# Row maxima of two attention stages as one stream over all units, ahead of the scores

## The chip, the cores and the metric

The kernel runs on one core of a Trainium2 chip (trn2). The metric is the device time of one execution in microseconds. The kernel before takes 6175.1 us, the median of three runs (6174.22 to 6192.93). The engines of the core are named as in the profile: PE (TensorE, matrix products), DVE (VectorE), ACT (ScalarE), POOL (GpSimd) and SP (SyncE, which only issues DMAs here). [...]

## The reference

The program is a whole decoder of four layers over 1024 tokens of 128 features. Each layer has a self-attention, a cross-attention to 6404 context rows, and a feed-forward part. Two of its twelve parts matter here. The first self-attention (layer 0) is causal, with 16 heads of size 8 and rotary positions:

```
q, k, v = x @ W_Q.T, x @ W_K.T, x @ W_V.T        (16 heads of 8, q and k rotated)
scores  = q @ k.T / sqrt(8), masked causally
x       = x + softmax(scores) @ v @ W_O.T
```

The last cross-attention (layer 3) has no causal mask, 6404 keys, and a mask over the keys:

```
q = Q @ Wq.T + bq;  k = ctx @ Wk.T + bk;  v = ctx @ Wv.T + bv
scores = where(mask == 0, -1e9, q @ k.T / sqrt(8))
ctx    = softmax(scores) @ v;   out = ctx @ Wo.T + bo
```

A softmax over 6404 keys needs the maximum of each row of scores before the exponentials. The kernel computes the scores twice: once with queries on the partitions, to find the row maxima, and once with keys on the partitions, for the exponentials and the product with the values.

## The kernel before

**Units.** Both stages work in eight units. A unit is a group of four heads (`g`, 0 to 3) and one half of the queries (`h`, 512 of them). The cross-attention takes unit n as g = n // 2, h = n % 2, the self-attention as g = n % 4, h = n // 4. A float32 query and key of size 8 are split into three bfloat16 parts, and stacked into 64 rows for each head (`split`, `pairs_read`), so one PE row group of 64 serves one head. Two heads share a tile of 128 partitions, which the code calls a pair. The key side has ones in three extra rows. Into the same rows of the query tile `qP` the negative maximum is added, as three parts, so that the second product yields scores less maximum at once.

**The maxima** of a unit come from `pairs_max`. A step is 128 queries against 512 keys for both pairs: per pair two matrix products into a PSUM tile `m2` of two banks, and one DVE reduction of 128 x 1024 scores to two maxima a row (L1275). In the cross-attention a unit has 13 chunks of keys times 4 query tiles, 52 steps; the last chunk has 260 keys. In the self-attention a unit has 4 steps in the first half of the queries and 8 in the second, with the causal mask added by two more products where a step meets the diagonal.

**The turn.** After the last step `pairs_neg` reduces over the chunks (L1285), splits the negative maximum into three parts with nine small DVE operations (L1285 to L1291) and writes them into the padded tile `mpad`. PE then turns `mpad` with four transposes for each pair (L1295), and DVE adds the result to the unit's part of `qP` (L1297).

**The scores.** `pairs_core` runs over the key tiles of a unit, 51 in the cross-attention and 4 or 8 in the self-attention. A tile has four score products into three single-bank PSUM tiles `s`, four exponentials on ACT (L1347), and four products with the values into `acc`, one tile late. The argument `beside` is the stream of steps for the next unit's maxima: the first pair of each tile is followed by one step, and what is left is run after the last tile. Then `acc` is copied to `oT`, on DVE and ACT in turn (L271, L273), and `pairs_norm` transposes it (L1368) and divides by the sums (L1371, L1373).

So the order around each boundary between units is: last value products, left-over steps, the negative maxima, the transposes of `mpad` and `oT`, the addition to `qP`, and only then the first scores of the next unit:

```
for n in range(7):
    g, h = n // 2, n % 2
    oT = pool1.tile([P, BANK], F32, tag="oT", name="oT")
    self.pairs_core(ps, pool1, qPs[g], kPs[g % 2], v, g, h, oT, AF.Exp, 64, maxima(n + 1))
```

The first unit's maxima run ahead of all scores: in the cross-attention in a prelude of 52 steps, among which `all_values` computes the values, in the self-attention in 4 steps. The eighth unit of the cross-attention has no maxima beside it and runs in a wider form (two banks to an exponential, L1344).

**What sets the order.** The matrix products made with `self.matmul` (L265) stay in the order of the program on PE. A scheduler places the rest: the small operations on DVE, the transposes, and the work of `between`, which in the self-attention replaces context rows that the first mask leaves out (L584 on DVE, L593 on ACT, L594 on POOL) and computes keys of the next stage (L599). In the cross-attention two tiles of keys `kP` serve in turn; the read of the next group is issued after the second unit of a group.

Of the kernel before, what the change touches and what calls it, by code (L numbers as in the profile page):

```python
# [10 lines left out]
F32 = mybir.dt.float32  # L11
# [3 lines left out]
AF = mybir.ActivationFunctionType  # L15
# [4 lines left out]
P = 128  # L20
# [191 lines left out]
class Decoder:  # L212
# [251 lines left out]
    def l0_attn(self):  # L464
# [9 lines left out]
        with tc.tile_pool(name="a", bufs=2) as pool:  # L474
# [41 lines left out]
            with tc.tile_pool(name="a1", bufs=2) as pool1, tc.tile_pool(name="a1_ps", bufs=2, space=PSUM) as ps0:  # L516
                ps = _Psum(ps0, m2=2, s=3, acc=1)
                steps = steps(ps)

                def maxima(n):  # L520
                    if n < 8:
                        return self.pairs_max(ps, pool1, qPs[n % 4], kPs[n % 4], n // 4, mpad, S, causal)
                    return ()

                for step in maxima(0):
                    step(0)
                    step(1)
# [725 lines left out]
    def pairs_max(self, ps, pool, qP, kP, h, mpad, nk=NK, causal=None):  # L1253
# [7 lines left out]
        for c in range(chunks):  # L1261
            for t in range(4):
                q0 = h * BANK + t * P
                a, b = c * BANK, min((c + 1) * BANK, nk if causal is None else q0 + P)

                def step(pair, a=a, b=b, q0=q0, t=t, c=c):
                    diag = causal is not None and b == q0 + P
                    m = ps.tile([P, 2, BANK], F32, tag="m2", name="m2")
                    for j in range(2):
                        r = slice(64 * j, 64 * j + 64)  # L1270
                        self.matmul(m[:, j, :b - a], lhsT=qP[pair][r, q0:q0 + P], rhs=kP[pair][r, a:b], start=True, stop=not diag)
                    if diag:
                        for j in range(2):
                            self.matmul(m[:, j, b - a - P:b - a], lhsT=causal[:, 1, :], rhs=causal[:, 0, :], start=False, stop=True)
                    nc.vector.tensor_reduce(mx[:, t, 2 * pair:2 * pair + 2, c:c + 1], m[:, :, :b - a], AX.X, ALU.max)  # L1275

                yield step
        self.pairs_neg(ps, pool, qP, h, mpad, mx)

    def pairs_neg(self, ps, pool, qP, h, mpad, mx):  # L1280

        nc = self.nc
        r = pool.tile([P, 4, 4], F32, tag="r", name="r")
        part = pool.tile([P, 4, 4], BF16, tag="part", name="part")
        nc.vector.tensor_reduce(r, mx, AX.X, ALU.max, negate=True)  # L1285
        mp = mpad.rearrange("p a t (j r) -> p t a j r", r=64)
        for i in range(3):
            nc.vector.tensor_copy(part, r)
            nc.vector.tensor_copy(mp[:, :, :, :, 7 + 8 * i], part.rearrange("p t (a j) -> p t a j", a=2))
            if i < 2:  # L1290
                nc.vector.tensor_tensor(r, r, part, ALU.subtract)  # L1291
        m = ps.tile([P, 2, BANK], F32, tag="m2", name="m2")
        for pair in range(2):
            for t in range(4):
                nc.tensor.transpose(m[:, pair, t * P:(t + 1) * P], mpad[:, pair, t, :], self.ident)  # L1295
            q = qP[pair][:, h * BANK:(h + 1) * BANK]
            nc.vector.tensor_tensor(q, q, m[:, pair, :], ALU.add)  # L1297

    def pairs_core(self, ps, pool, qP, kP, v, g, h, oT, func, rows, beside=None, between=None, causal=None):

# [20 lines left out]
        for t in range(nkt):  # L1321
# [1 line left out]
            off = 0 if causal is None else max(t * P - h * BANK, 0)  # L1323
            w, hs = BANK - off, slice(h * BANK + off, (h + 1) * BANK)
            diag = causal is not None and t >= 4 * h
            step = next(beside, None)
            ws = []
            for pair in range(2):
                both = None
# [16 lines left out]
                    for j in range(2):  # L1346
                        nc.scalar.activation(pp[j][:n, :w], ss[j][:n, :w], func)  # L1347
                ws += pp
                if step and pair == 0:
                    step(0)  # L1350
                    step(1)
            if late:
                values(*late.pop(0))
            late.append((t, n, off, ws))
            if between is not None:
                next(between, None)
        values(*late.pop(0))
        for step in beside:
            step(0)
            step(1)  # L1360
        self.copy(oT, acc)

    def pairs_norm(self, ps, pool, oT, o, g, h):
# [391 lines left out]
    def l3_xattn(self):  # L1755
# [5 lines left out]
        with tc.tile_pool(name="x", bufs=2) as pool:  # L1761
# [28 lines left out]
            with tc.tile_pool(name="x1", bufs=2) as pool1, tc.tile_pool(name="x1_ps", bufs=2, space=PSUM) as ps0:  # L1790
                ps = _Psum(ps0, m2=2, s=3, acc=1)

                def maxima(n):
                    if n < 8:
                        return self.pairs_max(ps, pool1, qPs[n // 2], kPs[n // 2 % 2], n % 2, mpad)
                    return ()
# [109 lines left out]
```

## Time and profile before

| What | us |
|---|---|
| Median of three runs | 6175.1 |
| The profiled execution, its own time | 6182.17 |
| Its span | 6180.4 |
| Granted PE clock over the span | 0.944 of full |
| First self-attention, units | 66 to 277 |
| Cross-attention, prelude of the first unit's maxima | 4870 to 4990 |
| Cross-attention, units 0 to 6 with maxima beside | 4990 to 5891 |
| Cross-attention, unit 7 alone | 5891 to 5987 |

The profile is of one execution. Times in it are counted from the start of its span. A row of the timeline gives start and length in us, engine, line and operation, the tile written and those read, partitions by elements, and a count of merged instructions; in brackets stand the idle time before it and what ended that. The table of stretches gives for each engine the busy time and the number of instructions, then the granted PE clock as a share of the full one. A line number can be that of a helper: all products made with `self.matmul` show as L265, so the tile's name tells them apart (`m` maxima, `s` scores, `acc` values).

Over the whole span PE is busy 5749.6 us, DVE 3757.0, ACT 3096.5 and POOL 2254.1. Most of that belongs to stages that the change leaves alone.

### The profile page before, as it was taken

Reading aid. Unit: us, or ns where it says so; the run is one execution under the profiler, and the core shown is the slowest. Engines: PE = TensorE matmul, PEld = TensorE weight load, DVE = VectorE, ACT = ScalarE, POOL = GpSimd, SP = SyncE. Lnnn points to the kernel's source line nnn. Section 1 sums busy time; section 2 is a strip of 40 time slices with the busy share of each in tenths; the row PEclk is TensorE's granted clock in tenths of the full one; section 3 lists DMA queues with packets and bytes.
Section 4 is the critical chain, followed back from the end, with each engine's and each line's share of the span. In section 5 each row is a group of like instructions: output and inputs, shape, how many; then the busy total and the mean of one; then the engine's idle time right before and its main releaser. Section 6 shows DMA issues by size and latency. Waiting matters only on the chain. (4 is left out here: it accounts for less than half of the span.)

```text
span 6180.4 us, 72184 instructions
## 1 busy us (share of the span) xinstructions
PE 5749.6 (93%) x29144; PEld 2078.1 (34%) x29144; DVE 3757.0 (61%) x4571; ACT 3096.5 (50%) x4041; POOL 2254.1 (36%) x1088
## 2 busy tenths in 40 slices
PE   5899999999999999999899968999989689999999
PEld 2333333333333434333476423111124311111126
DVE  6587777777777777776325552100014799999923
ACT  2434444444444444444211225899951167888872
POOL 2057767677777767678321541100001000000000
PEclk7899999999999999999979977999999689999999
DMA  3000000000000000000000013200022100000000
GB/s 113 4 1 1 1 1 1 1 1 1 1 1 1 1 1 1 1 17 18 33 1 14 0 58 87 88 11 7 1 83 80 54 1 22 1 22 1 1 6 29
DMA packets 65200, 117.97 MB, mean 19 GB/s; under 512 B 10475, under 2 KB 46673, under 8 KB 63201
## 3 DMA queue, kind: packets, MB, share of 16 engines
q1 hardware_dynamic: 64288, 110.08, 5.5%
q8 instruction: 228, 3.74, 0.3%
q10 hardware_dynamic: 576, 3.28, 0.1%
q14 instruction: 108, 0.88, 0.0%
HBM read 81.88 MB, written 31.42 MB: 18 GB/s over the span
## 5 line engine op out<-in xcount | busy, mean ns | idle before, releaser
L741 POOL TENSOR_TENSOR tot<-tot,p 128x1024 f32<-128x1024 f32 (+1 forms) x800 | 1889.8, 2362 | 584.5 <-ACT p L732 569.0
L732 ACT ACTIVATE p<-p,drop,keep 128x1024 f32<-128x1024 f32 (+1 forms) x816 | 1011.8, 1240 | 1321.7 <-DVE p L731 1260.0
L669 DVE TENSOR_REDUCE mx<-m 128x2 f32<-128x1024 f32 (+1 forms) x832 | 982.4, 1185 | 496.3 <-PE m L668 479.8
L1275 DVE TENSOR_REDUCE mx<-m 128x2 f32<-128x1024 f32 (+4 forms) x928 | 1027.1, 1159 | 93.5 <-PE m L265 82.2
L731 DVE TENSOR_TENSOR p<-s,every 128x1024 f32<-128x1024 f32 (+1 forms) x816 | 991.5, 1215 | 73.2 <-PE s L726 34.7
L1347 ACT ACTIVATE p<-s 128x512 f32<-128x512 f32 (+4 forms) x1620 | 819.7, 588 | 238.8 <-PE s L265 238.0
L668 PE MATMUL m<-kT,qT 64*128 64x512 f32 (+1 forms) x3328 | 888.6, 606 | 12.3 <-DVE mx L669 11.6
L1344 ACT ACTIVATE p<-s 128x1024 f32<-128x1024 f32 x918 | 843.9, 1185 | 31.5 <-PE s L1339 24.1
L726 PE MATMUL s<-qT,kT 64*128 64x512 f32 (+1 forms) x3264 | 837.7, 596 | 16.6 <-DVE p L731 15.4
L713 PE MATMUL acc<-p,v 128*64 128x512 f32 (+1 forms) x3264 | 809.4, 606 | 4.8 <-ACT p L732 3.8
L1318 PE MATMUL acc<-p,v 128*8 128x512 f32 (+2 forms) x3672 | 621.9, 597 | 0.0
L265 PE MATMUL m<-kP,qP 64*128 64x512 bf16 (+4 forms) x1856 | 371.5, 396 | 102.7 <-DVE mx L1275 57.0
L726 PEld LDWEIGHTS s<-qT,kT 64*128 64x128 f32 (+1 forms) x3264 | 321.7, 185 | 412.5 <-issue 342.1
L668 PEld LDWEIGHTS m<-kT,qT 64*128 64x128 f32 x3328 | 280.7, 185 | 504.1 <-DVE mx L669 371.4
L265 PE MATMUL acc<-p,v 128*9 128x512 f32 (+2 forms) x3240 | 422.2, 593 | 0.0
L265 PE MATMUL s<-qP,kP 64*128 64x512 bf16 (+4 forms) x1620 | 384.0, 387 | 8.9 <-ACT p L1347 6.2
L713 PEld LDWEIGHTS acc<-p,v 128*64 128x64 f32 (+1 forms) x3264 | 198.8, 136 | 550.9 <-issue 457.9
L1339 PE MATMUL s<-qP,kP 48*128 48x512 bf16 (+2 forms) x1836 | 281.0, 384 | 2.7 <-ACT p L1344 1.9
L271 DVE COPY oT<-acc 128x512 f32<-128x512 f32 x14 | 9.7, 690 | 404.4 <-PE acc L1318 395.7
L387 POOL MEMSET mpad<- 128x512 f32 x2 | 1.1, 529 | 641.2 <-PE m L1428 600.4
L265 PEld LDWEIGHTS <-qP 64*128 64x128 bf16 x1856 | 122.7, 96 | 319.6 <-issue 261.9
L265 PEld LDWEIGHTS <-kP 64*128 64x128 bf16 (+1 forms) x1620 | 83.7, 94 | 352.3 <-issue 347.4
(484 smaller groups left out, 4512.5 us busy)
## 6 DMA issues: line engine op xcount, KB each, us to landing
kd<-part SPq DMA_DIRECT2D x156, 128.0 KB, 1.9
wb<-expert_weights SPq DMA_DIRECT2D x30, 512.0 KB, 3.7
kP<-kd SPq DMA_DIRECT2D x24, 512.0 KB, 3.6
kP<-kd SPq DMA_DIRECT2D x48, 192.0 KB, 4.5
w_expert<-in_Y_w SPq DMA_DIRECT2D x8, 768.0 KB, 4.2
qd<-part SPq DMA_DIRECT2D x36, 128.0 KB, 1.8
qP<-qd SPq DMA_DIRECT2D x16, 256.0 KB, 6.2
ctxT<-in_ctxT ACTq DMA_DIRECT2D x4, 800.5 KB, 6.5
```

Source lines behind the costliest of these rows:

```text
L265: return self.tc.keep_in_program_order(self.nc.tensor.matmul(*a, **k))
L668: nc.tensor.matmul(m[:, j, :b - a], lhsT=qT[r, q0:q0 + P], rhs=kT[r, a:b], start=True, stop=True)
L669: tc.keep_in_program_order(nc.vector.tensor_reduce(mx[:, t, :, c:c + 1], m[:, :, :b - a], AX.X, ALU.max))
L713: nc.tensor.matmul(acc[64 * j:64 * j + 64, :], lhsT=v[:n, t, 64 * j:64 * j + 64], rhs=pr[:n, j, :], start=t == 0, stop=t == NKT - 1, tile_ ...
L726: nc.tensor.matmul(s[:n, j, :], lhsT=kT[r, t * P:t * P + n], rhs=qT[r, hs], start=True, stop=True)
L731: tc.keep_in_program_order(nc.vector.tensor_tensor(pr[:n], s[:n], every[:n], ALU.add))
L732: nc.scalar.activation(pr[:n], pr[:n], AF.Exp, bias=drop[:n, t:t + 1], scale=keep[:n, t:t + 1])
L741: nc.gpsimd.tensor_tensor(tot[:n], tot[:n], pr[:n], ALU.add)
L1275: nc.vector.tensor_reduce(mx[:, t, 2 * pair:2 * pair + 2, c:c + 1], m[:, :, :b - a], AX.X, ALU.max)
L1318: matmul(acc[32 * j:32 * j + v.shape[3], off:], lhsT=v[:n, t, 4 * g + j, :], rhs=ws[j][:n, :BANK - off], start=t == 0, stop=t == nkt - 1, ...
L1344: nc.scalar.activation(p2[:n], both[:n], func)
L1347: nc.scalar.activation(pp[j][:n, :w], ss[j][:n, :w], func)
```

## The change

The steps of all eight units become one stream. `pairs_max` no longer runs the turn at its end: it returns its steps and a function that starts it. `pairs_neg` does the small DVE operations when called and returns a second function, `turned`, with the transposes and additions. A new function, `maxima_of`, joins the units: after the last step of a unit it issues the small operations, then yields the next unit's first step, and issues `turned` after it. The transposes of `mpad` now stay in program order on PE.

`pairs_core` takes the stream and a number of steps for the unit and spreads these over its tiles. With 52 steps over 51 tiles the last tile has two, the second of them after its second pair. Nothing is left over at the end of a unit.

The stream starts early: in the cross-attention 56 steps run in the prelude, 52 of the first unit and 4 of the second, and every unit then takes 52 (the seventh finds 48). In the self-attention 6 run ahead, and the units take 4, 4, 6, 8, 8, 8, 8 and 8 as far as there are any. A unit's turn thus comes inside the unit before it: in the cross-attention in front of the second maxima of the tile that has the first step of the unit after.

```diff
-                def maxima(n):
-                    if n < 8:
-                        return self.pairs_max(ps, pool1, qPs[n % 4], kPs[n % 4], n // 4, mpad, S, causal)
-                    return ()
-
-                for step in maxima(0):
+                maxima = self.maxima_of(self.pairs_max(lambda: ps, pool1, qPs[n % 4], kPs[n % 4], n // 4, mpad, S, causal)
+                                        for n in range(8))
+                for _ in range(6):
+                    step = next(maxima)
                     step(0)
                     step(1)
...
-                    self.pairs_core(ps, pool1, qPs[g], kPs[g], v, g, h, oT, AF.Exp, 64, maxima(n + 1), steps, causal)
+                    self.pairs_core(ps, pool1, qPs[g], kPs[g], v, g, h, oT, AF.Exp, 64,
+                                    (maxima, 4 if n < 2 else 6 if n == 2 else 8), steps, causal)
...
-        self.pairs_neg(ps, pool, qP, h, mpad, mx)
+        return steps(), lambda: self.pairs_neg(banks, pool, qP, h, mpad, mx)
...
-        m = ps.tile([P, 2, BANK], F32, tag="m2", name="m2")
-        for pair in range(2):
-            for t in range(4):
-                nc.tensor.transpose(m[:, pair, t * P:(t + 1) * P], mpad[:, pair, t, :], self.ident)
-            q = qP[pair][:, h * BANK:(h + 1) * BANK]
-            nc.vector.tensor_tensor(q, q, m[:, pair, :], ALU.add)
+
+        def turned():
+            m = banks().tile([P, 2, BANK], F32, tag="m2", name="m2")
+            for pair in range(2):
+                for t in range(4):
+                    self.tc.keep_in_program_order(nc.tensor.transpose(m[:, pair, t * P:(t + 1) * P], mpad[:, pair, t, :], self.ident))
+                q = qP[pair][:, h * BANK:(h + 1) * BANK]
+                nc.vector.tensor_tensor(q, q, m[:, pair, :], ALU.add)
+
+        return turned
+
+    def maxima_of(self, units):
+
+        late = None
+        for steps, neg in units:
+            for i, step in enumerate(steps):
+                yield step
+                if i == 0 and late:
+                    late()
+                    late = None
+            late = neg()
+            if i == 0:
+                late = late()
+        if late:
+            late()
...
-        beside = iter(beside or ())
+        beside, count = beside or (iter(()), 0)
...
-            step = next(beside, None)
+            mine = range(count * (t + 1) // nkt - count * t // nkt)
...
-                if step and pair == 0:
-                    step(0)
-                    step(1)
+                for _ in mine[pair::2]:
+                    step = next(beside, None)
+                    if step:
+                        step(0)
+                        step(1)
...
-        for step in beside:
-            step(0)
-            step(1)
         self.copy(oT, acc)
...
+            maxima = self.maxima_of(self.pairs_max(lambda: ps, pool, qPs[n // 2], kPs[n // 2 % 2], n % 2, mpad) for n in range(8))
...
-                for step in self.pairs_max(ps, pool0, qPs[0], kPs[0], 0, mpad):
+                for _ in range(52 + 4):
+                    step = next(maxima)
                     step(0)
                     step(1)
                     next(vs, None)
...
-                    self.pairs_core(ps, pool1, qPs[g], kPs[g % 2], v, g, h, oT, AF.Exp, 64, maxima(n + 1))
+                    self.pairs_core(ps, pool1, qPs[g], kPs[g % 2], v, g, h, oT, AF.Exp, 64, (maxima, 52))
```

More of the change, by code (lines that the diff above doesn't have):

```diff
@@ L1251, in pairs_read, with pairs_max @@
                 self.nc.sync.dma_start(out=t[:, a:b], in_=src[at:at + 16, :, a:b].rearrange("p i c -> (p i) c"))
-    def pairs_max(self, ps, pool, qP, kP, h, mpad, nk=NK, causal=None):
+    def pairs_max(self, banks, pool, qP, kP, h, mpad, nk=NK, causal=None):
         nc = self.nc
@@ L1260, in pairs_max, with steps, step, pairs_neg @@
         mx = pool.tile([P, 4, 4, chunks], F32, tag="mx", name="mx")
-        for c in range(chunks):
-            for t in range(4):
[L1263 to L1267, printed above, removed]
-                    m = ps.tile([P, 2, BANK], F32, tag="m2", name="m2")
[L1269 to L1272, printed above, removed]
-                        for j in range(2):
-                            self.matmul(m[:, j, b - a - P:b - a], lhsT=causal[:, 1, :], rhs=causal[:, 0, :], start=False, stop=True)
-                    nc.vector.tensor_reduce(mx[:, t, 2 * pair:2 * pair + 2, c:c + 1], m[:, :, :b - a], AX.X, ALU.max)
-                yield step
-        self.pairs_neg(ps, pool, qP, h, mpad, mx)
-    def pairs_neg(self, ps, pool, qP, h, mpad, mx):
+        def steps():
+            for c in range(chunks):
+                for t in range(4):
+                    q0 = h * BANK + t * P
+                    a, b = c * BANK, min((c + 1) * BANK, nk if causal is None else q0 + P)
+                    def step(pair, a=a, b=b, q0=q0, t=t, c=c):
+                        diag = causal is not None and b == q0 + P
+                        m = banks().tile([P, 2, BANK], F32, tag="m2", name="m2")
+                        for j in range(2):
+                            r = slice(64 * j, 64 * j + 64)
+                            self.matmul(m[:, j, :b - a], lhsT=qP[pair][r, q0:q0 + P], rhs=kP[pair][r, a:b], start=True, stop=not diag)
+                        if diag:
+                            for j in range(2):
+                                self.matmul(m[:, j, b - a - P:b - a], lhsT=causal[:, 1, :], rhs=causal[:, 0, :], start=False, stop=True)
+                        nc.vector.tensor_reduce(mx[:, t, 2 * pair:2 * pair + 2, c:c + 1], m[:, :, :b - a], AX.X, ALU.max)
+                    yield step
+        return steps(), lambda: self.pairs_neg(banks, pool, qP, h, mpad, mx)
+    def pairs_neg(self, banks, pool, qP, h, mpad, mx):
         nc = self.nc
@@ L1291, in pairs_neg @@
                 nc.vector.tensor_tensor(r, r, part, ALU.subtract)
-        m = ps.tile([P, 2, BANK], F32, tag="m2", name="m2")
-        for pair in range(2):
-            for t in range(4):
-                nc.tensor.transpose(m[:, pair, t * P:(t + 1) * P], mpad[:, pair, t, :], self.ident)
-            q = qP[pair][:, h * BANK:(h + 1) * BANK]
-            nc.vector.tensor_tensor(q, q, m[:, pair, :], ALU.add)
+        def turned():
+            m = banks().tile([P, 2, BANK], F32, tag="m2", name="m2")
+            for pair in range(2):
+                for t in range(4):
+                    self.tc.keep_in_program_order(nc.tensor.transpose(m[:, pair, t * P:(t + 1) * P], mpad[:, pair, t, :], self.ident))
[6 more added lines that the diff above has]
+            for i, step in enumerate(steps):
+                yield step
+                if i == 0 and late:
[6 more added lines that the diff above has]
+            late()
     def pairs_core(self, ps, pool, qP, kP, v, g, h, oT, func, rows, beside=None, between=None, causal=None):
@@ L1791, in l3_xattn @@
                 ps = _Psum(ps0, m2=2, s=3, acc=1)
[L1793 to L1796, printed above, removed]
                 for n in range(7):
```

## The prediction

> **What bounds the kernel now.** The page's slices first: TensorE (PE) is over nine tenths busy nearly everywhere, so a share of busy time decides nothing; the change touches two stretches, found by following the `qP` and `oT` tiles in time: the first self-attention, 53 to 280 us, and the last cross-attention, 4870 to 5990 us. Next the busy time by stretch (stretch, length, then PE, weight loads, VectorE (DVE), ScalarE (ACT), GpSimd (POOL), granted PE clock):
>
> ```profile
> 66.00:248.00 182.00, 147.40 (x993) 53.98 (x992) 122.61 (x220) 87.62 (x190) 15.59 (x13) 0.83 0.00 1
> 248.00:280.00 32.00, 29.28 (x126) 6.71 (x125) 1.81 (x4) 15.25 (x34) 0.00 (x0) 0.50 0.00 1
> ...
> 5249.00:5364.00 115.00, 109.43 (x776) 21.29 (x772) 114.34 (x99) 101.05 (x196) 0.00 (x0) 1.00 0.00 1
> 5364.00:5378.00 14.00, 10.10 (x66) 3.84 (x64) 7.86 (x21) 5.39 (x11) 0.00 (x0) 0.82 0.00 1
> ```
>
> Inside a cross-attention unit (115 us) DVE is busy 114.34: it bounds, with row maxima. Only the 14 us between units have room, 6.1 us of DVE. In the self-attention neither engine is full and the clock is 0.83, then 0.50. The timeline of one boundary shows where the room is (start, length, work, idle before):
>
> ```profile
> 5364.66 1.31 DVE L1275 TENSOR_REDUCE mx<-m 128x2 f32<-128x520 f32 x2 [1.03 <-PE m L265]
> 5367.10 1.31 DVE L1275 TENSOR_REDUCE mx<-m 128x2 f32<-128x520 f32 x2 [1.14 <-PE m L265]
> 5370.23 1.31 DVE L1275 TENSOR_REDUCE mx<-m 128x2 f32<-128x520 f32 x2 [1.82 <-PE m L265]
> ...
> 5375.03 0.69 DVE L1297 TENSOR_TENSOR qP<-qP,m 128x512 bf16<-128x512 bf16 x1 [1.27 <-PE m L1295]
> ...
> 5376.93 0.69 DVE L1297 TENSOR_TENSOR qP<-qP,m 128x512 bf16<-128x512 bf16 x1 [0.46 <-PE m L1295]
> 5377.90 114.05 DVE L1275 TENSOR_REDUCE mx<-m 128x2 f32<-128x1024 f32 x98 [0.28 <-PE m L265]
> ```
>
> ```profile
> 5369.90 0.40 PE L265 MATMUL m<-kP,qP 64*128 64x260 bf16 x4
> 5373.91 1.09 PE L1295 MATMUL m<-ident,mpad 128*128 128x128 f32 x4 [3.61 <-DVE mpad L1289]
> 5374.79 1.06 PE L1368 MATMUL m<-ident,oT 128*128 128x128 f32 x4
> 5375.77 1.12 PE L1295 MATMUL m<-ident,mpad 128*128 128x128 f32 x4
> ```
>
> PE stands 3.6 us for the nine small DVE operations that put -max into `mpad`; the second four transposes begin only after the first add. DVE itself idles 1.03+1.14+1.82 before the short maxima (260 columns of keys) and 2.2 us around the adds: 6.2 in all.
>
> **The cross-attention, one unit (128.5 us, from 5249.58 to 5377.90 to 5506.38).** Not one maxima operation is removed: 416 steps before and after. So DVE keeps its sum: 96 full reductions at 1.175 = 112.8, 8 short at 0.655 = 5.2, the -max chain 1.75, two adds 1.38, normalisation and clearing 1.0, half a copy 0.35: 122.5. Only idle time can go. The new order:
> - 44 full tiles at 2.35 = 103.4, then the 4 short tiles. There the loop score, exp, score, values also takes 2.35 (scores start at 5361.76, 5364.11, 5366.46), so DVE waits 1.03 three times: 1.31 + 7.04. They end at 111.7.
> - The chain, now on DVE between two full reductions, ends 4.1 later. PE, which arrives at 3.5, waits 0.65; then transposes, add, transposes, add in one string. With the clock at full, four transposes take 0.7 (the row 211.13 in the self-attention says 0.63; the 1.09 above are at half clock). DVE idles 0.9 and 0.8. All this is queued in front of the tile's second scores and of the older tile's value products.
> - The last tile now has two steps, 4 full reductions: DVE ends at 14.25. PE's 16 value products end at 14.35, copy 0.65, transposes 0.7, new scores, first reduction at 16.45: 1.2 idle.
>
> Sum 111.7+16.45 = 128.15, DVE idle 6.0 against 6.2. **The unit gains 0.3 us, practically nothing**: what leaves the boundary comes back as a stall inside the unit. Five inner units: -2.
>
> Ends of the stage: the prelude makes 4 steps more, 8 reductions at 1.13 = 9, with the turn in between: first unit's reductions begin 15.5 after the 52nd step against 6.9, +8.6; the first unit's start-up idle (1.15+1.21) is then covered, -2.2. The seventh unit has 48 steps only, but its tiles don't get shorter, for the 2.35 loop remains; it hands over 124.5 after its begin against 127.7, -3.2; the eighth starts at full clock, -1.5. Stage: **about 0**, bounds -15 (all idle goes) and +20 (below).
>
> **The self-attention.** Here PE waits most:
>
> ```profile
> 112.53 1.09 PE L1295 MATMUL m<-ident,mpad 128*128 128x128 f32 x4 [8.86 <-DVE mpad L1289]
> ...
> 178.76 1.09 PE L1295 MATMUL m<-ident,mpad 128*128 128x128 f32 x4 [3.26 <-DVE mpad L1289]
> ...
> 211.13 0.63 PE L1295 MATMUL m<-ident,mpad 128*128 128x128 f32 x4 [1.97 <-DVE mpad L1289]
> ...
> 258.34 0.58 PE L265 MATMUL s<-qP,kP 64*128 64x512 bf16 x1 [0.26 <-ACT p L1347]
> 258.85 1.89 PE L265 MATMUL acc<-p,v 128*9 128x512 f32 x8
> ```
>
> From the last value product to the next unit's scores it takes 9.0, 11.8, 6.0, 12 (with four left-over steps), 6.2, 4.5, 5.4 us. After: a turn inside the unit (0.7+0.75+0.7, add and slot 0.3: 2.5) and at the boundary a wait for the copy and the transposes (0.8+0.8): 4.1. The wait for `mpad` lies behind some 2.5 us of scores and values.
> - Start: two more steps before the first scores, +2.6.
> - Unit 0: the context sums (L584, 0.69 each) are scheduled between the chain's small operations, six of them; PE still waits some 3: 7.8 against 9.0, -1.2. Unit 1: the chain runs beside the POOL additions, where small DVE rows take 1.2 to 1.3 us; 10.8 against 11.8, -1.0.
> - Unit 2 gets six steps: DVE 13.6 for maxima, 4.1 for the rest, 1 idle: 18.7 against 17.1, +1.6. Unit 3, eight steps in four tiles, nothing left over: 20.9 against 22.2, -1.3.
> - Units 4, 5, 6: boundary -2.0, -0.3, -1.2; slow-clock rows at their start (155, 181 to 188, 213) gone, -1, -2.1, -1; diagonal maxima beside full scores +0.8 in unit 4; four steps fewer in unit 6, -1.6. Together -8.4.
> - Unit 7 (29.1 us, no maxima) runs whole at half clock: eight value products 1.89 against 1.05. At full clock its four full tiles need 2.35, the diagonal ones about 2: 21. -8.
>
> Sum: 2.6-1.2-1.0+1.6-1.3-8.4-8 = **-15.7**.
>
> Here a rule is weighed against rows. The Trainium skill, "TensorE: Matmul & The Clock Gate", "What's actually happening", has the clock return after one busy window, about 3.4 us. Then unit 7 would have recovered by 255 and keeping it warm would be worth 2: sum -10. But the row 248 to 280 has PE 92% busy and the clock at 0.50 throughout. I take the row: -8. The same section lets the clock fall only after an idle window; the clock rows show it fall at 147 us with PE 70% busy from 143 to 147. That speaks against the change: its stalls are shorter but twice as many. For unit 7 I take full clock, since after the cross-attention boundaries windows that the PE rows show 76 to 83% busy kept it.
>
> SP's and POOL's queues keep every instruction in its place; the `kP` reads still stand a whole unit before their first use, even four steps earlier. One more `m2` slot in use for the turn is in the sums (second step waits for the second add).
>
> **Total**: 0 - 15.7, rounded -16. The profiled execution took 6182.2 (span 6180.4, 1.8 around it): 6166; it lies 7.1 above the median 6175.1, so **6159**.
>
> **Rivals.**
> 1. *The stream fills DVE's idle in the cross-attention too* (22%). For it: DVE has 6 us idle per unit. Against: 3 of them come from the 2.35 us loop. At half of it in five units, -12 more: 6147.
> 2. *The gain is hidden* (15%): unit 7 stays at half clock, as it does for 34 us now. -8: 6167.
> 3. *The turn's wait drops the PE clock* (13%), slower. In the last three tiles of a cross-attention unit PE idles 0.65+0.75 and then 0.7; if a window counts as idle, 16 value products take 1.7 more, scores and maxima 0.6, transposes 1.1: +3.4 in each of six units, +20, with the start's +6.4 and -3.2 of the end, and the self-attention left with -3: +20, 6195. It decides when nearly every unit is hit; at half of them it is +10. For it: the fall at 147. Against: PE is some 80% busy in these windows.
> 4. *The order isn't what it says* (5%): DVE might do the chain before older maxima; but the built order has the turn behind the next unit's first step. About 6175.
>
> **Chances.** 0.3% (18.5 us) is what a measurement can tell from no change. The forecast case has 45% and its own range 6150 to 6168, two fifths of it beyond 6156.6. Faster 0.18+0.22 = 0.40; slower most of rival 3, 0.10; the same 0.50. Range 6140 to 6186.
>
> **What would show it.** PE's wait before the `mpad` transposes under 1 us in the cross-attention, 3.6 now; a unit of 128 us, DVE idle 6; clock 1.00 across boundaries, and unit 7 of the self-attention near 21 us. Wrong if a cross-attention unit takes 125 or 132, or the clock dips after the turn.

## The result and the profile after

The changed kernel takes 6217.16 us, the median of four runs (6215.03 to 6217.61). The kernel before took 6182.56 us beside it on the same chip (four runs, 6174.22 to 6192.93). The ratio is 1.0057, with a 95% interval of 1.0042 to 1.0071: it is slower, by 35 us, where the forecast had 16 us the other way. The profiled execution took 6217.26 us (span 6215.4, 6180.4 before). The executions of one kernel differ (49 of the kernel before, run beside one group of the experiments, spread over 33 us), so a trace, which is of one execution, need not show what the median does.

Busy time by stretch of the changed kernel, with the columns of the table shown before (stretch, length, then PE, weight loads, DVE, ACT, POOL, granted clock). The four stretches are, roughly, the self-attention's first seven units, its last unit, the inside of a cross-attention unit, and the 25 us around a boundary with the turn in it:

```profile
66.00:252.00 186.00, 152.70 (x951) 48.67 (x950) 118.66 (x214) 85.98 (x184) 15.70 (x13) 0.78 0.00 1
252.00:282.00 30.00, 25.68 (x148) 5.54 (x146) 1.88 (x5) 16.80 (x39) 0.00 (x0) 0.77 0.00 1
5275.00:5370.00 95.00, 91.11 (x648) 17.48 (x640) 94.81 (x82) 83.34 (x162) 0.00 (x0) 1.00 0.00 1
5375.00:5400.00 25.00, 20.13 (x120) 4.37 (x116) 16.33 (x26) 13.03 (x25) 0.00 (x0) 0.82 0.00 1
```

The inside of a unit is as before: DVE 94.81 of 95 us, full clock. PE is busy 152.70 us in the self-attention's first seven units for much the same work as the 147.40 before, at a clock of 0.78 for 0.83. So the loss is to be sought at the boundaries. The PE rows of one of them, between the third and the fourth unit (start, length, line and operation, tiles, count, idle before):

```profile
5384.15 0.39 PE L265 MATMUL s<-qP,kP 64*128 64x512 bf16 x2
5385.27 0.63 PE L1301 MATMUL m<-ident,mpad 128*128 128x128 f32 x4 [0.73 <-DVE mpad L1293]
5386.68 0.66 PE L1301 MATMUL m<-ident,mpad 128*128 128x128 f32 x4 [0.78 <-DVE qP L1303]
5387.27 0.39 PE L265 MATMUL m<-kP,qP 64*128 64x512 bf16 x2
5388.12 0.61 PE L265 MATMUL m<-kP,qP 64*128 64x512 bf16 x2 [0.46 <-DVE qP L1303]
5388.50 0.65 PE L265 MATMUL s<-qP,kP 64*128 64x512 bf16 x2
5389.08 1.89 PE L265 MATMUL acc<-p,v 128*9 128x512 f32 x8
...
5393.06 0.39 PE L265 MATMUL m<-kP,qP 64*128 64x512 bf16 x2 [0.60 <-DVE mx L1278]
5394.19 0.39 PE L265 MATMUL m<-kP,qP 64*128 64x512 bf16 x2 [0.74 <-DVE mx L1278]
5394.51 3.66 PE L265 MATMUL acc<-p,v 128*9 128x512 f32 x16
5398.96 1.11 PE L1390 MATMUL m<-ident,oT 128*128 128x128 f32 x4 [0.78 <-ACT oT L273]
```

The turn does what it was forecast to do: PE waits 0.73 us for `mpad` (3.6 before), its transposes take 0.63 and 0.66 at full clock. Then the price appears. Two matmuls that took 0.39 at 5387.27 take 0.61 at 5388.12, eight value products take 1.89 (1.05 at full clock), and sixteen take 3.66. The clock has been halved, as the pieces further down show. DVE's rows of the same place (waits 0.81 and 0.75 at the additions, where the prediction had 0.9 and 0.8) show who waits for it in turn:

```profile
5385.94 0.69 DVE L1303 TENSOR_TENSOR qP<-qP,m 128x512 bf16<-128x512 bf16 x1 [0.81 <-PE m L1301]
5387.38 0.69 DVE L1303 TENSOR_TENSOR qP<-qP,m 128x512 bf16<-128x512 bf16 x1 [0.75 <-PE m L1301]
5387.98 2.35 DVE L1278 TENSOR_REDUCE mx<-m 128x2 f32<-128x1024 f32 x2
5391.78 4.62 DVE L1278 TENSOR_REDUCE mx<-m 128x2 f32<-128x1024 f32 x4 [1.45 <-PE m L265]
5399.09 0.48 DVE L1330 MEMSET acc<- 128x512 f32 x1 [2.68 <-ACT oT L273]
```

The reductions behind the turn now wait 1.45 us for PE, and at the unit's end DVE idles 2.68 behind the sixteen slow value products and the copy. The same stretch in pieces of 3.41 us, which is how long the trace's clock records hold a value at the least:

```profile
5384.40:5387.81 3.41, 1.75 (x12) 0.95 (x11) 1.85 (x4) 1.08 (x2) 0.00 (x0) 1.00 0.00 0
5387.81:5391.22 3.41, 3.10 (x14) 0.34 (x13) 2.52 (x3) 1.08 (x2) 0.00 (x0) 0.50 0.00 0
5391.22:5394.63 3.41, 2.07 (x16) 0.59 (x18) 2.85 (x3) 2.02 (x4) 0.00 (x0) 1.00 0.00 0
5394.63:5398.05 3.42, 3.42 (x16) 0.12 (x9) 1.77 (x2) 0.00 (x0) 0.00 (x0) 0.50 0.00 0
```

In the first piece PE is busy 1.75 of 3.41 us, 51%, because both waits of the turn fall in it. The next runs at half clock and is 91% busy, and behind it the clock returns. Then come the two waits for a reduction (0.60, 0.74), PE is busy 61%, and the clock falls again just ahead of the sixteen value products; this time it stays down for four pieces, until 5408.3.

The stage in parts, from the end of the 52nd step to the last unit's reciprocal, and the time per unit at half clock, from the clock records (mean of the second to sixth unit). A unit here runs from one reciprocal of `pairs_norm` to the next, the first from the first exponential:

| us | front | first unit | next five | seventh | eighth | sum | half clock a unit |
|---|---|---|---|---|---|---|---|
| before | 7.7 | 128.1 | 642.1 | 127.9 | 99.2 | 1005.1 | 6.2 |
| after | 16.5 | 132.6 | 660.2 | 127.0 | 98.1 | 1034.4 | 13.9 |

So 29 of the 35 us are lost here: 8.8 ahead of the first exponential, 4.5 in the first unit, 18.1 in the next five, while the last two give back 2.1. The front, in PE rows of the changed kernel:

```profile
4992.55 1.09 PE L1301 MATMUL m<-ident,mpad 128*128 128x128 f32 x4 [3.91 <-DVE mpad L1293]
4994.41 1.11 PE L1301 MATMUL m<-ident,mpad 128*128 128x128 f32 x4 [0.78 <-DVE qP L1303]
4995.46 1.46 PE L265 MATMUL m<-kP,qP 64*128 64x512 bf16 x6
...
5003.10 0.61 PE L265 MATMUL s<-qP,kP 64*128 64x512 bf16 x2 [2.79 <-DVE mx L1278]
```

Between the turn and the first scores stand the reductions of the three steps drawn ahead behind it.

In the self-attention the eighth unit's reciprocal comes at 282.1 (277.1 before): 10.6 us are lost by the end of the seventh unit (257.4 for 246.9), most of it in the third and fourth unit (24.0 and 26.7 us for 17.1 and 22.2), and 5.6 won in the eighth (24.7 for 30.2). The layers between are the same code, and end within 1 us of where that leaves them.

### The profile page after: what moved, and what is told of

Same layout as the page of the kernel before. It is cut to its first block, busy times and chain, and to the rows that moved or that the text cites. A ratio compares the mean times of both kernels' runs of the same rounds, so it can differ in the third digit from the quotient of the medians.

```text
span 6215.4 us, 72180 instructions
## 1 busy us (share of the span) xinstructions
PE 5781.8 (93%) x29144; PEld 2069.9 (33%) x29144; DVE 3752.9 (60%) x4571; ACT 3097.2 (50%) x4041; POOL 2254.4 (36%) x1088
## 5 line engine op out<-in xcount | busy, mean ns | idle before, releaser
L265 PE MATMUL acc<-p,v 128*9 128x512 f32 (+2 forms) x3240 | 439.0, 617 | 0.0
L265 PE MATMUL s<-qP,kP 64*128 64x512 bf16 (+4 forms) x1620 | 393.0, 395 | 15.7 <-ACT p L1370 10.5
## 6 DMA issues: line engine op xcount, KB each, us to landing
kd<-part SPq DMA_DIRECT2D x156, 128.0 KB, 1.8
qd<-part SPq DMA_DIRECT2D x36, 128.0 KB, 1.8
```

The source lines that it names most:

```text
L265: return self.tc.keep_in_program_order(self.nc.tensor.matmul(*a, **k))
```

## The experiments

**Theory: the clock.** The turn and the unit's end put several short waits into one piece of time, the clock is halved behind them, and the work that follows takes up to twice as long. **Rivals:** the waits themselves cost the time; or the steps drawn ahead do. Each run was timed beside the kernel before, whose median was 6180 to 6182 us in all four groups of runs. Kernels are built on the kernel before, with the changed functions used only in the stage named.

### Each stage alone

```diff
-                    self.pairs_core(ps, pool1, qPs[g], kPs[g % 2], v, g, h, oT, AF.Exp, 64, maxima(n + 1))
+                    self.pairs_core_s(ps, pool1, qPs[g], kPs[g % 2], v, g, h, oT, AF.Exp, 64, (maxima, 52))
```

The last cross-attention alone:

> The change is made in the last cross-attention alone; the first self-attention stays as before. From the two profiles the 35 us split as about +4 in the self-attention, +1 in the layers between (whose code is the same) and +29 from the cross-attention's prelude on. Both theories of the cross-attention (the clock falls behind the turn; the four steps drawn ahead are not paid back) expect +28 to +30 over before. A theory that the self-attention's own loss is larger, because later stages inherit a colder clock from it, expects at most +20.

The first self-attention alone:

> The change is made in the first self-attention alone. By the profiles: +4 to +6 over before (the last reciprocal of the stage came 5.0 us later in the changed kernel, the layer norm after it 3.6). The prediction had -16 here; if the profiled self-attention was an unlucky draw of the clock, the median comes out between -16 and 0.

Measured: 6209.56 us for the cross-attention alone, ratio 1.0042 (1.0029 to 1.0054), +28.5. The self-attention alone took 6188.21, ratio 1.0012 (1.0005 to 1.0018), +7.2. Together 35.7: the two stages add up, and no large part comes from one through the other.

### Matmuls that keep PE busy

Twelve matmuls without use in each turn and norm, into banks that are written over or never read:

```diff
             for pair in range(2):
+                for i in range(4 if pair == 0 else 0):
+                    self.matmul(m[:, 0, :], lhsT=kP[0][:, 0:P], rhs=kP[0][:, 0:BANK], start=True, stop=True)
                 for t in range(4):
                     self.tc.keep_in_program_order(nc.tensor.transpose(m[:, pair, t * P:(t + 1) * P], mpad[:, pair, t, :], self.ident))
+                for i in range(4 if pair == 0 else 0):
+                    self.matmul(m[:, 1, :], lhsT=kP[0][:, 0:P], rhs=kP[0][:, 0:BANK], start=True, stop=True)
...
+            for i in range(4):
+                self.matmul(m[:, 1, :], lhsT=busy[:, 0:P], rhs=busy[:, 0:BANK], start=True, stop=True)
```

> The cross-attention of the change with twelve matmuls added in each turn and norm, into banks that are overwritten or never read: four ahead of the first four transposes, four between the two groups of four, four ahead of the norm's transposes. The order of everything else is that of the change. If the clock falls because TensorE stands idle in short waits there, the windows fill up, the half-clock stretches behind the turns (some 17 us in a unit) shrink to before's 7, and the units that took 131 to 133 us come back to about 129: -10 to -16 against the cross-only kernel. If the waits themselves and not the clock cost the time, the added matmuls can only add: 0 to +12 (84 matmuls of at most 0.43 us that lie partly in waits).

Measured: 6187.89 us, ratio 1.0012 (1.0006 to 1.0019), 22 us less than without them. Work was added and the kernel became faster. PE rows at the same boundary, of the kernel with the added matmuls (those `m<-kP` with 128*128):

```profile
5371.31 1.04 PE L265 MATMUL m<-kP 128*128 128x512 bf16 x3
5372.18 0.60 PE L1413 MATMUL m<-ident,mpad 128*128 128x128 f32 x4
5372.62 1.03 PE L265 MATMUL m<-kP 128*128 128x512 bf16 x4
5374.43 0.66 PE L1413 MATMUL m<-ident,mpad 128*128 128x128 f32 x4 [0.78 <-DVE qP L1417]
...
5380.85 2.02 PE L265 MATMUL acc<-p,v 128*9 128x512 f32 x16
5382.80 1.04 PE L265 MATMUL m<-kP 128*128 128x512 bf16 x3
5383.67 0.63 PE L1510 MATMUL m<-ident,oT 128*128 128x128 f32 x4
```

The sixteen value products take 2.02 us, not 3.66; the wait of 0.78 is still there. By stretch:

```profile
5264.00:5359.00 95.00, 90.99 (x650) 17.60 (x648) 95.00 (x82) 83.45 (x163) 0.00 (x0) 1.00 0.00 1
5364.00:5389.00 25.00, 21.03 (x140) 5.70 (x144) 19.64 (x30) 15.25 (x30) 0.00 (x0) 1.00 0.01 1
```

The boundary has a clock of 1.00 for 0.82, and from the second unit on the stage has no record of half clock. Each of the five units takes 128.5 us. The added matmuls stand where PE waited and give DVE nothing earlier, and the waits for the addition and for the reductions are still in the trace with 0.4 to 0.8 us. So the clock theory holds, and the rival that the waits themselves cost the time falls.

### Which waits

Both groups of transposes ahead of both additions:

```diff
             for pair in range(2):
                 for t in range(4):
                     self.tc.keep_in_program_order(nc.tensor.transpose(m[:, pair, t * P:(t + 1) * P], mpad[:, pair, t, :], self.ident))
+            for pair in range(2):
                 q = qP[pair][:, h * BANK:(h + 1) * BANK]
```

> The cross-attention of the change with the eight transposes of a turn issued before its two additions, so that the second group of four no longer waits for the first addition (0.78 us in the profile). Straight bookkeeping of the wait: 7 x 0.8 = -5 against the cross-only kernel. Clock theory: if that wait is what brings the window under what keeps the clock, -10 to -16; if the other waits of the boundary suffice to bring it down, -3 to -6 only.

Measured: 6190.66 us, ratio 1.0013 (1.0004 to 1.0023), 19 less than the change in the cross-attention alone. That is four times the bookkeeping of the wait and more than the 10 to 16 of the clock theory. In the trace, units of 127.6 us with 1 to 2 us at half clock stand beside units of 130.6 with 10.

The added matmuls in the turn only:

> The cross-attention of the change with the eight added matmuls in the turn only, none at the norm. In the profile of the change the clock falls twice at most boundaries: behind the turn (window with 52 to 56% of TensorE busy) and again 7 us later at the unit's end (window with 61%), where it stays down for four windows. If the second fall follows from the first (everything is late after a window at half clock), this one kernel is as good as that with all twelve: units 128.5. If the unit's end drops the clock by itself: units about 131, half-clock time 10 to 14 us each.

Measured: 6199.75 us, ratio 1.0032 (1.0019 to 1.0044); units 130.7 to 132.6, half clock 8 to 13 us each. So 10 of the 22 us come with the turn's matmuls alone, and the unit's end drops the clock by itself. At the norm only (the four matmuls of the last hunk above alone):

> The counterpart: the four added matmuls at the norm only, none in the turn. If the turn's fall is the cause of the other: units 131 to 133 as in the change. If the unit's end is what costs: the first fall stays (one window of 3.4 us), the second goes, units 129 to 130, half-clock time 3 to 7 us each.

Measured: 6187.89 us, ratio 1.0012 (1.0003 to 1.0021), by the median as good as all twelve. But its executions lie in two groups, six of 6176 to 6182 us and seven of 6188 to 6196, and the one profiled took 6181.32: what the upper group does is not known. In this trace three of the five units take 127.6 to 127.8 us with at most 0.3 at half clock, the other two 131.8 and 130.5.

The turn, where nothing was added, drops the clock at one of the first six boundaries here, and at five of these six in the change. What differs is where the pieces begin. Two of them at the turn between the third and fourth unit, whose transposes start at 5368.60 and 5370.01 us:

```profile
5365.30:5368.71 3.41, 2.64 (x19) 0.55 (x16) 3.09 (x9) 2.87 (x6) 0.00 (x0) 1.00 0.00 0
5368.71:5372.13 3.42, 2.18 (x18) 1.04 (x22) 2.11 (x3) 0.34 (x2) 0.00 (x0) 1.00 0.00 0
```

One wait lies in each piece, PE is busy 77% and 64%, and the clock holds. In the change a piece begins 0.9 to 1.2 us ahead of the turn's first transposes at all six boundaries, holds both waits and is 51 to 56% busy. Here only two boundaries are aligned like that, and the clock fell at one of them. The turns of the change follow each other after 129.5 or 133.1 to 133.3 us, within 0.2 us of 38 or 39 pieces; in the kernel with matmuls at the norm they come 127.5 to 132.1 us apart, and the alignment moves. A likely reason is that the clock changes only where a piece begins: what runs after the return is then in step with the pieces, and the next turn meets them where the last one did. No run tests this.

The norm put off until behind the next unit's first tile, both groups of transposes first, two steps ahead, nothing added:

```diff
-                    self.pairs_core_s(..., (maxima, 52))
+                    self.pairs_core_s(..., (maxima, 52), norm_of(unit))
...
-                    self.pairs_norm(ps, pool1, oT, o, g, h)
+                    unit = (ps, pool1, oT, o, g, h)
```

> No matmul is added. The cross-attention of the change with both groups of transposes ahead of both additions, two steps drawn ahead, and the norm of a unit issued behind the first tile of the next one instead of at the unit's end, so that the first scores of a unit no longer stand behind transposes that wait for the copy. If the wait for the copy is what drops the clock at the boundary, the units run at the full clock without help (126.5 to 128 us, half-clock time under 3 us each) and the kernel comes to -5 to +2 against before. If the turn's waits alone suffice to drop it, as before the boundary itself is only 0.8 us shorter: units 130 to 132, +10 to +18.

Measured: 6190.26 us, ratio 1.0012 (1.0003 to 1.0021). Every unit takes 129.7 to 129.9 us with 10.2 to 10.4 at half clock, so the result lies between the two expectations. Its PE rows show a new wait that the edit itself makes:

```profile
5372.66 0.57 PE L265 MATMUL s<-qP,kP 64*4 64x512 bf16 x2
5375.29 1.07 PE L1411 MATMUL m<-ident,mpad 128*128 128x128 f32 x8 [2.05 <-DVE mpad L1403]
```

With two steps ahead the turn falls into the last tile, which has only four keys, and PE has nothing to bridge the wait for `mpad` with: 2.05 us. So the same with four steps ahead:

> The deferred norm with four steps drawn ahead instead of two, so that the turn stands three tiles ahead of the unit's end again; no added matmul. The front costs 4.3 more. If it was the nearness of the turn to the unit's end that made a window of 41%, and the copy's wait is what counts otherwise: half-clock time under 5 us a unit, units 127 to 128, so -5 to -8 over the stage after its front against the two-step version. If the turn's waits drop the clock alone: the units stay at 129 to 130 and the kernel is 4 slower than the two-step version.

Measured: 6186.35 us, ratio 1.0011 (1.0004 to 1.0017). Two units still take 129.8 with 10 us at half clock, three 127.7 to 128.4 with 2 to 5. Neither expectation is met as a whole: in this trace the same code keeps the clock in some units and loses it in others.

### The steps drawn ahead

The twelve added matmuls keep the clock of the units steady, so that the front can be weighed, with `range(52 + 2)` for `range(52 + 4)` in the prelude:

> The kernel of the cross-attention with added matmuls (which held the full clock through the whole stage), with two steps drawn ahead in the prelude instead of four. What that kernel still loses lies ahead of the first unit: its units take 128.5 us as before's do and the last ones are 4.5 us shorter, yet it is 7 us slower in all. If each step drawn ahead costs the prelude more than it saves at the end (by the profiles some 2 us a step at the front), two fewer bring -4 to -5 against it. If the front is long for another reason (the wait of the first scores for the turn), the two steps bring nothing: -1 to +1.

Measured: 6184.62 us, ratio 1.0005 (0.9996 to 1.0013), 3.3 less by the medians of two groups of runs. In the traces the front shrinks from 18.2 to 13.7 us, and the seventh and eighth unit take the same 125.7 and 97.0. Each step ahead costs 2.3 us at the front, and from two to four none comes back.

With both groups of transposes first as well:

> The two-step lead, the added matmuls, and both groups of transposes ahead of both additions, in the cross-attention alone. By the waits: another 7 x 0.4 to 0.8 = -3 to -5 against the two-step kernel; if the added matmuls already fill that wait without costing, 0. Against the kernel before: -2 to +3 if before's units lose nothing to the clock, and as much below the kernel before with added matmuls as the last units are shorter (about -4).

Measured: 6179.95 us, ratio 0.9997 (0.9990 to 1.0003): no difference from the kernel before. The units take 128.0 us.

### The same matmuls in the kernel before

> The kernel before, with the same twelve matmuls added to the turn and the norm of each unit of the last cross-attention and nothing else changed. If the clock is what the boundaries cost, before loses by it too (5 to 9 us at half clock in each unit): -1.5 to -3 a unit, -10 to -20 in all. If before's dips lie in time that the vector or scalar engine fills anyway, only the added matmuls are seen: 0 to +6.

Measured: 6208.98 us, ratio 1.0043 (1.0030 to 1.0056), 27 slower; neither expectation was near. A unit takes 132.3 us for 128.4, with 8.9 us at half clock for 6.2. PE rows of one boundary of it:

```profile
5382.23 1.02 PE L265 MATMUL m<-kP 128*128 128x512 bf16 x4 [0.69 <-DVE mx L1275]
5385.07 1.11 PE L1297 MATMUL m<-ident,mpad 128*128 128x128 f32 x4 [1.82 <-DVE mpad L1289]
5385.98 1.91 PE L265 MATMUL m<-kP 128*128 128x512 bf16 x4
5388.67 1.12 PE L1297 MATMUL m<-ident,mpad 128*128 128x128 f32 x4 [0.78 <-DVE qP L1301]
5389.58 1.91 PE L265 MATMUL m<-kP 128*128 128x512 bf16 x4
```

Four matmuls do not fill its wait for `mpad` (0.69 and 1.82 us are left), the clock falls all the same, and the other eight then lie on the path at 1.91 us for four. Here filler helped where it reached over the wait, and cost where it did not.

### The self-attention

The change there alone, with the twelve matmuls:

> The self-attention of the change alone, with the same twelve matmuls in each turn and norm there. If the lengthening of the third and fourth unit (24 and 27 us for before's 17 and 22) is the clock's, which falls in the turns, the half-clock share up to 200 us shrinks and the kernel gains 5 to 15 us against the self-only kernel. If these units are held by the vector engine, whose reductions were moved into them, nothing is gained and the matmuls add: 0 to +6.

with them and both groups of transposes first:

> The change in the self-attention alone, with the twelve added matmuls and both groups of transposes ahead of both additions. If the order of the transposes is what the kernel with both stages gains over the sum of its parts: -11 to -15 against before. If the parts interact (a steadier clock in one stage carries into the other): -2 to -4, as without the new order.

and with both groups first, nothing added:

> The change in the self-attention alone with both groups of transposes ahead of both additions and no added matmul. If the wait for the first addition is what drops the clock there: 0 to -10 against before, third and fourth unit at 22 us. If the chain of reductions and casts ahead of the transposes suffices to drop it: +3 to +8 as in the change, third and fourth unit 23 and 27 us.

Measured in this order: 6179.25 us, ratio 0.9994 (0.9987 to 1.0000); 6164.28, ratio 0.9978 (0.9970 to 0.9986); 6169.70, ratio 0.9987 (0.9979 to 0.9995). So -2.4, -16.0 and -10.6 against before, where the change alone had +7.2. The order of two additions and four transposes turns the stage's loss into a gain, at the edge of the 0 to -10 expected. But the 22 us expected of its third and fourth unit are not met: in its trace they take 22.6 and 26.6 us, the fourth with 17 us at half clock, and it is the second, with 19.2 us for 26.1 before, that makes up for them. Where the median's gain comes from is therefore not shown for this kernel. Busy time from 113.5 to 185 us, from the third unit on: of the kernel before, of the self-only kernel, and of that with the new order and the added matmuls:

```profile
113.50:185.00 71.50, 58.24 (x425) 23.78 (x424) 53.57 (x90) 29.48 (x70) 0.00 (x0) 0.83 0.00 1
```

```profile
113.50:185.00 71.50, 55.51 (x347) 17.79 (x336) 47.53 (x79) 27.09 (x60) 4.49 (x4) 0.70 0.00 1
```

```profile
113.50:185.00 71.50, 59.93 (x450) 22.62 (x449) 56.22 (x91) 28.27 (x67) 0.00 (x0) 0.95 0.00 1
```

The clock is 0.95 for 0.70 (0.83 before), and DVE gets 56.22 us of work done for 47.53. By unit ends, in us from the span's start:

| kernel | seventh unit's end | eighth unit |
|---|---|---|
| before | 246.9 | 30.2 |
| self-attention changed alone | 257.8 | 20.1 |
| with added matmuls | 246.1 | 20.4 |
| both groups first, added matmuls | 247.0 | 20.1 |
| both groups first, nothing added | 245.9 | 28.8 |

The 11 us lost up to the seventh unit come back with either mend, but no more than that (in the eleven traces whose self-attention is that of before this end lies between 242.6 and 247.8). The gain over the kernel before lies in the eighth unit, which has no maxima beside it. In the kernel before a turn stands at its head, and PE waits for it:

```profile
245.32 0.63 PE L1295 MATMUL m<-ident,mpad 128*128 128x128 f32 x4 [2.92 <-DVE mpad L1289]
```

In all eleven traces PE is busy 14 to 36% of the piece with this wait, and the clock falls behind it. The unit then takes 30.2 to 30.3 us nine times, and 21.3 and 22.7 where the clock came back early. The stream takes the turn away from there. In four of the six traces with the changed self-attention the clock holds and the unit takes 20.1 to 20.4 us; in the change itself it falls behind a piece of 71% and in the last kernel of the table behind one of 58%. The kernel with added matmuls was profiled in an execution of 6167.35 us (median 6179.25), the last of the table in one of 6179.81 (median 6169.70), so the medians of these two cannot be read from their traces.

### Both stages mended

> Both stages of the change, each with the twelve added matmuls in turn and norm and both groups of transposes ahead of the additions, two steps drawn ahead in the cross-attention. If the two stages add up: -2.4 (self-attention with added matmuls) -1.7 (cross-attention) = -4 against before, -1 to -8 with what the free second addition saves in the self-attention. If the gains of the self-attention come only of a lucky clock: about -2.

Measured: 6166.49 us, ratio 0.9976 (0.9967 to 0.9984), -15, well beyond the -1 to -8 expected. It beats both kernels, but all of it is the self-attention's (-16.0 with the same edits alone, in another group of runs): in the cross-attention the stream brings nothing clear of the noise even at full clock. The best version without added work is the self-attention with both groups first and the cross-attention left alone, -10.6.

## Why the prediction was wrong

**The clock in the cross-attention: the step that failed.** The sum held at full clock: "The unit gains 0.3 us, practically nothing" gave 128.15, and the units with the clock held take 128.5. What failed is that the forecast put the clock's loss at nothing: it reckoned "With the clock at full" and set the third rival aside with "PE is some 80% busy in these windows", about the share at which it had seen the clock kept behind the boundaries of before (76 to 83%). The prediction's own figures said otherwise: 0.65 and 0.75 us of idle follow each other within 1.5 us, and a piece of 3.41 us that holds both is at most 59% busy. Measured were 51% and then 61%, and the clock fell behind both. The rival's place (the turn, and after it the sixteen value products, transposes and scores) was right, and so was its size: "+3.4 in each of six units", +20, stands against 22 us that holding the clock brought back. It had 13% and should have been the forecast. Its whole sum, +20, is still short of the 35: it had the self-attention at -3, which came at +7, and front and ends together at +3, which came at +7.

**The front and the ends: mis-sized.** "+8.6" for the steps ahead was right (8.8). "-2.2" for a start-up idle that would be covered did not come: even in the kernel with twelve added matmuls the first unit takes 1.5 us more than before's. The end, "-3.2" and "-1.5", measured -2.4 and -2.2 in that kernel, -1.0 and -1.2 in the change itself. With the clock held the stage is 7.8 us longer than before's (1012.9 for 1005.1, of which the added matmuls in the prelude's turn make 1.7), where the sum had "about 0".

**The self-attention.** "-15.7" measured +7.2. The -8 for "Unit 7", from half to full clock, came as -5.6 in the change and as -10 in the four kernels whose eighth unit kept the clock, as the forecast had it; before's own unit escapes most of the half clock in two traces of eleven. What failed is the rest, -7.7, which took durations at the clock that before's rows had: the third and fourth unit were put at +1.6 and -1.3 and came at +6.9 and +4.4 in the profile, and units five to seven at -1.1 for the -8.4. With either mend units one to seven together end as before (-1.0 to +0.1 us, not -7.7). That a wait inside a unit replaces the one at its boundary, as the prediction had found for the cross-attention, would explain this; it was not tested apart.

**The rule weighed.** The prediction set the Trainium skill's rule ("TensorE: Matmul & The Clock Gate", "What's actually happening": a fall after an idle window, a return after a busy one) against the rows and took the rows, for the direction of one unit only. The same page, under "A second HAM failure mode: psum-queue depth-cycling", says that a PE which idles briefly but often makes the clock swing. That fits what happened here, with no gap over 0.8 us at this boundary, and it spoke against this change. By the first rule, if idle means a window without work, nothing would have been lost at this boundary; holding the clock brought back 22 us.

## What to carry to other kernels

Before moving a wait, add up TensorE's idle time in any 3.4 us around its new place, wherever they may begin, not over a tile or a boundary: here two waits of 0.7 to 0.8 us in one piece cost more through the clock than through their own length. Order instructions so that the waits do not alternate with short bursts of matmuls (here all eight transposes before both additions), which was worth 18 us in one stage and 19 in the other. Work drawn ahead costs its full length at the front; here the last two units repaid 4.5 us of it, no more for four steps than for two.

## What was not expected of the hardware

The trace's clock records last 3.41 us or a whole number of such pieces. Counted from 4990 to 5890 us, in the cross-attention's first seven units, in all 17 traces (before, after and the experiments), by TensorE's busy share in a piece and whether the clock is other in the next one:

```
busy share    at full clock: pieces, falls    at half clock: pieces, returns
under 50%             34, 34                          22, 0
50 to 59%             23, 16                           6, 0
60 to 69%             77, 25                          13, 0
70 to 79%             86, 10                          31, 0
80 to 89%            166, 7                           27, 13
90% and more        3856, 0                          139, 88
```

There is no single threshold in this count: between 50 and 90% the clock may fall or hold; a return came only behind pieces of 80% and more, and in 88 of 139 cases at 90% and more. Some matmul records can be missing from a trace, and only the matmuls' busy time is counted, so the shares are rough. What decides between a fall and none at the same share was not tried. Nor was it settled why parts with the same code differ by 4 to 9 us between traces (from the layer norm at 4773 us in before, one part ahead of the cross-attention, to the end of the prelude's 52nd step, five traces take 205.7 to 207.2 us and twelve 210.3 to 211.0); part of the difference between two medians may be such draws.
